# 1/std by a power of -0.5 on GpSimd, for four sets of rows, in a two-layer attention kernel

## The chip, the core and the metric

The kernel runs on one core of a Trainium2 chip. The metric is the time of one execution on the device in microseconds (us), of which the median of several runs is given. Engines are named as in the profile: PE is TensorE, DVE is VectorE, ACT is ScalarE, POOL is GpSimd, SP is SyncE (here it only issues transfers).

## The reference

The input x has 4 batches of 1024 rows of 256 numbers. Four layers are applied, each to rows that are normalised first, and each is added to x. All is in fp32.

```
x = x + attn_a(layernorm(x))      # 16 heads of 64
x = x + ffn(layernorm(x))         # 256 -> 1024 -> 256, exact Gelu
x = x + attn_b(layernorm(x))      # attn_b normalises once more inside, with scale and bias,
                                  # and adds its own normalised input to its output
x = x + ffn(layernorm(x))         # same weights

layernorm: m, v = mean(x), mean((x - m)**2);  (x - m) / sqrt(v + 1e-5)
```

In `attn_b` the inner normalisation has rows that are already normalised, so its variance is the first variance times the square of the first 1/std. Both attentions are softmax(q k^T) v with the heads' outputs multiplied by an output matrix; the second one rotates q and k by position.

## The kernel before

x stays in SBUF for the whole program, as four tiles of 128 partitions with 8 row tiles of 256 columns each. A *block* is half a batch: 512 rows, four row tiles. There are 8 blocks.

**Attention.** `attention` (it is called for both layers) goes through 256 steps: for each of 4 batches, for each of 8 pairs of heads, for each of 8 query tiles. For one step, PE computes the scores of both heads (L238, into PSUM), DVE takes the maximum of each row (L249), ACT the exponential with its row sum (L251), DVE the reciprocal of the sums (L259), ACT copies this into the same tile (L260), and DVE transposes the tile in squares of 32 by 32 (L271). Transfers between SBUF tiles then bring each square to its place (L295): most are issued by SP, five for each two steps by POOL. Some steps later PE multiplies the transposed exponentials by v (L304), ACT copies the sums (L314), POOL multiplies them by the reciprocals (L316), PE projects them (L167), ACT copies the projection (L326) and POOL adds it to x (L328). This second half is done for two steps at a time, so a pair of steps is the period of the work. The order on each engine is written out by hand in `steps_with`; what else has to be done within the attention (the projections of the next pair of heads, the rotation of q and k by POOL in L657 to L659, the normalisation of the next batch) is put into it as *pieces* that each have the number of a step, those of one number in the order in which they were handed in.

**Normalisation.** `scaling` makes tiles for a set of blocks: mean and variance of its rows (`mv`, one column pair for each row tile), `rstd`, `shift` and, for the second attention, `more`. `measure` (L126, L127, DVE) fills `mv`. `finish` works out the factors of the whole set at once: ACT takes the square root (L130), DVE the reciprocal (L131), then DVE the product with the mean and its sign (L137, L138). With `again` the second 1/std follows in the same manner (L133 to L136). `standardize` (L147, ACT) is what uses `rstd` and `shift`: one Identity with a scale and a bias for each row tile.

ACT's functions lie in tables. The program that is built has an `ACT_TABLE_LOAD` ahead of a function whose table isn't there: the square root, the exponential and Gelu each need one of their own; copies and Identity work with each of them.

`Rows` groups the blocks into sets of one layer, each with its own `finish`:

- layer a, `rows` in `layer_a`: block 0, block 1, and blocks 2 to 7. The third set (24 row tiles) is finished as a piece of step 28 of the first attention; its first use is at step 32.
- the two feed-forwards, names f and g: blocks 0 and 1, blocks 2 to 5, blocks 6 and 7. The first set (8 row tiles) is finished at step 254 (`n - 2` in `ffn_between`) of the attention before; `normed(0)` follows it in the same step and uses it at once: four Identities on ACT, each followed by an addition of the bias to x on POOL (L396). Then come transposes on PE (L153), the copies of them (L156), and the first matrix product with Gelu (`up`, L410 and L414).
- layer b, name b: the same sets as f, with `again`. The third set (8 row tiles) is finished at step 30 of the second attention and used for the last batch, from step 152 on.

Of the kernel before, what the change touches and what calls it, by code (L numbers as in the profile page):

```python
# [9 lines left out]
F32 = mybir.dt.float32  # L10
AF = mybir.ActivationFunctionType
ALU = mybir.AluOpType
# [3 lines left out]
P = 128  # L16
# [23 lines left out]
def hybrid_block_kernel(  # L40
# [5 lines left out]
    nc = tc.nc  # L46
# [3 lines left out]
    const = ctx.enter_context(tc.tile_pool(name="const", bufs=1))  # L50
# [26 lines left out]
    make_identity(nc, ident)  # L77
    eps = const.tile([P, 1], F32, name="eps")
    nc.vector.memset(eps, EPS)
    b1_sb = const.tile([P, NF], F32, name="b1_sb")  # L80
    lns_sb = const.tile([P, NC], F32, name="lns_sb")
    lnb_sb = const.tile([P, NC], F32, name="lnb_sb")
# [21 lines left out]
        nc.gpsimd.dma_start(lnb_sb, ln_b.rearrange("(c p) -> p c", p=P))  # L104


    def scaling(name, blocks, again=False):

        where = {}
        for b, qb in blocks:
            for t in range(TQ):
                where[b, qb * TQ + t] = len(where)
        m = len(where)
        mv = const.tile([P, m, 2], F32, name=f"{name}_mv")
        rstd = const.tile([P, m], F32, name=f"{name}_rstd")  # L120
        shift = const.tile([P, m], F32, name=f"{name}_shift")
        more = const.tile([P, m], F32, name=f"{name}_more") if again else None

        def measure(b, t):
            stats = small.tile([P, 6], F32, tag="stats", name="stats")
            nc.vector.bn_stats(stats, xs[b][:, t, :])  # L126
            nc.vector.bn_aggr(mv[:, where[b, t], :], stats)  # L127

        def finish():
            nc.scalar.activation(rstd, mv[:, :, 1], AF.Sqrt, bias=eps)  # L130
            nc.vector.reciprocal(rstd, rstd)  # L131
            if again:
                nc.vector.tensor_mul(more, mv[:, :, 1], rstd)  # L133
                nc.vector.tensor_mul(more, more, rstd)
                nc.scalar.activation(more, more, AF.Sqrt, bias=eps)
                nc.vector.reciprocal(more, more)  # L136
            nc.vector.tensor_mul(shift, mv[:, :, 0], rstd)  # L137
            nc.vector.tensor_scalar_mul(shift, shift, -1.0)  # L138

        def get(b, t):  # L140
            i = slice(where[b, t], where[b, t] + 1)
            return shift[:, i], rstd[:, i], more[:, i] if again else None

        return measure, finish, {k: (lambda k=k: get(*k)) for k in where}

    def standardize(dst, src, shift, rstd):
        nc.scalar.activation(dst, src, AF.Identity, scale=rstd, bias=shift)  # L147

    def transposed(dst, src, c, affine=None):

        tr = group(TQ, P)
        for t in range(TQ):
            nc.tensor.transpose(tr[:, t, :], src[:, t, ts(c, P)], ident)  # L153
        trf = tr.rearrange("p t q -> p (t q)")
        if affine is None:
            nc.scalar.copy(dst[:, c, :], trf)  # L156
        else:
            nc.scalar.activation(
                dst[:, c, :], trf, AF.Identity,
                scale=affine[0][:, c : c + 1], bias=affine[1][:, c : c + 1],  # L160
            )
# [204 lines left out]
    blocks = [(b, qb) for b in range(B) for qb in range(NQB)]  # L366

    class Rows:


        def __init__(self, name, sets, again=False):
            self.finish, self.get, self.by = [], {}, {}
            for i, which in enumerate(sets):
                measure, finish, get = scaling(f"{name}{i}", which, again)
                self.finish.append(finish)
                self.get.update(get)
                self.by.update({k: measure for k in get})
# [114 lines left out]
    def layer_a():  # L492

        scale_a = 1.0 / (DH * DH * H)
        hTs = {}
        rows = Rows("a", (blocks[:1], blocks[1:2], blocks[2:]))

        def batch_a(b):
            work = []
            for qb in range(NQB):  # L500
                k = {}

                def straight(t, b=b, k=k, qb=qb):
                    if t == 0:
                        k["xn"] = xnp.tile([P, TQ, D], F32, tag="xn", name="xn")
                    dst, src = k["xn"][:, t, :], xs[b][:, qb * TQ + t, :]
                    shift, rstd = rows.factors(NQB * b + qb, t)[:2]
                    if b == 0 and qb == 1:
                        nc.vector.tensor_scalar(dst, src, rstd, shift, op0=ALU.mult, op1=ALU.add)
                    else:  # L510
                        standardize(dst, src, shift, rstd)

                def turned(c, b=b, k=k, qb=qb):
                    if c == 0:
                        p, tag = ((lowp, "low"), (highp, f"high{b % 2}"))[qb]
                        hTs[b, qb] = p.tile([P, NC, QB], F32, tag=tag, name="hT")
                    transposed(hTs[b, qb], k["xn"], c)

                work += [(10 * qb + t, lambda t=t, f=straight: f(t)) for t in range(TQ)]
                work += [(10 * qb + 6 + 2 * c, lambda c=c, f=turned: f(c)) for c in range(NC)]  # L520
            return work

        def pair_a(b, pr):
            made = {}

            def load():
                w = made["w"] = wp.tile([P, 3, NC, P], F32, tag="w", name="w")
                for i in (1, 0, 2):
                    nc.gpsimd.dma_start(
                        w[:, i], wqkv_a[i, :, ts(pr, P)].rearrange("(c p) f -> p c f", p=P)  # L530
                    )

            def qk(i, qb):
                name = ("qT", "kT")[i]
                if qb == 0:
                    made[name] = qkp.tile([P, S], F32, tag=name, name=name)
                pq = group(QB)
                paired(pq, [
                    (made["w"][:, i, c, :], [hTs[b, qb][:, c, :]] * 2) for c in range(NC)
                ])  # L540
                dst = made[name][:, ts(qb, QB)]
                if i == 0:
                    nc.scalar.mul(dst, pq, scale_a)
                else:
                    nc.scalar.copy(dst, pq)

            def values(m):
                if m == 0:
                    made["v"] = vp.tile([P, NK2, DH], F32, tag="v", name="v")
                pv = group(4, DH)  # L550
                for t in range(4):
                    qb, tt = divmod(4 * m + t, QB // DH)
                    by_head(pv[:, t, :], [
                        (hTs[b, qb][:, c, ts(tt, DH)], made["w"][:, 2, c, :]) for c in range(NC)
                    ])
                nc.scalar.copy(made["v"][:, ts(m, 4), :], pv)

            work = [(4 - 4 * i + 2 * qb - EARLY, lambda i=i, qb=qb: qk(i, qb)) for i in (1, 0) for qb in range(NQB)]
            work += [(6 + 2 * m, lambda m=m: values(m)) for m in range(NT // 2)]
            return {name: lambda name=name: made[name] for name in ("qT", "kT", "v")}, load, work  # L560


        later = [(4 + i, lambda i=i: rows.measure(2 + i // TQ, i % TQ)) for i in range(6 * TQ)]
        later += [(4 + 6 * TQ, lambda: rows.finish[2]())]
        first, steps = attention(batch_a, pair_a, wo_a, nc.gpsimd, lead=3, kept=0)
        loads, xn, pair = first[:2], first[2:14], first[14:]

        def measured(qb):
            for t in range(TQ):
                rows.measure(qb, t)  # L570
            rows.finish[qb]()

        def ready():

            nc.scalar.activation(small.tile([P, 1], F32, tag="nmax", name="ready"), eps, AF.Exp)


        first = loads + [lambda: measured(0)] + xn[:4] + [lambda: measured(1), ready] + xn[4:6] + pair[:1]
        first += xn[6:] + pair[1:3]
        later += [((-1, 0, 0, 1, 1)[i], f) for i, f in enumerate(pair[3:])]  # L580
        return first, lambda others: steps(later + others)
# [101 lines left out]
    n_steps = B * NF * NT  # L683
    sets = (blocks[:2], blocks[2:6], blocks[6:])
    first_a, steps_a = layer_a()
    rows_b = Rows("b", sets, again=True)
    first_b, steps_b = layer_b(rows_b)
    end_a, rest_a, ramp_b = ffn_between(Rows("f", sets), False, n_steps, rows_b, first_b)
    end_b, rest_b, _ = ffn_between(Rows("g", sets), True, n_steps)
    for f in first_a[:2]:  # L690
        f()
    load_rest()
# [63 lines left out]
```

## Time and profile before

| | |
|---|---|
| three runs | 3285.77, 3290.56, 3292.66 us; median 3290.56 |
| the profiled execution | 3286.08 us, of which 3284.2 are the span from the first to the last instruction |
| first attention and its start | about 0 to 1415 us |
| first feed-forward | about 1415 to 1560 us |
| second attention | about 1560 to 3030 us |
| second feed-forward | about 3030 to 3284 us |
| granted PE clock | 0.997 of full, mean over the span |
| ACT_TABLE_LOAD | 20, of 1283 ns each |
| square roots, L130 and L135 | 15, of about 0.3 us each |
| DVE reciprocals, L131 and L136 | 15, of 0.18 to 0.30 us each |

The first layers of the next stage overlap the end of the one before, so the limits of the stages are not sharp. In the profile's lines a time is given in us from the start of the span; an operation is named by its engine, its line in the kernel, what it writes and what it reads. Text in square brackets says how long the engine stood idle before it, and what ended that. Busy time of POOL is rough, and a PE that is shown busy isn't at its peak.

### The profile page before, as it was taken

How to read it: one execution, taken by the hardware profiler on the slowest of the kernel's cores; microseconds unless marked ns; L12 is line 12 of the kernel's file. 1: busy time of each engine (PE TensorE's matmuls, PEld its weight loads, DVE VectorE, ACT ScalarE, POOL GpSimd, SP SyncE). 2: the span in 40 equal slices, each digit the busy share in tenths (PEclk: the TensorE clock that was granted, in tenths of full speed). 3: DMA queues.
4: the chain of work that ended last, by engine and by line, in shares of the span. 5: the costliest groups of instructions: out<-in, count | busy, mean ns of one | idle time of the engine just before them, and what ended most of it. 6: DMA issues, size and time to landing. Idle time of an engine off the chain costs nothing.

```text
span 3284.2 us, 126564 instructions
## 1 busy us (share of the span) xinstructions
PE 3204.3 (98%) x52736; PEld 2022.2 (62%) x52736; DVE 2531.7 (77%) x2386; ACT 2107.9 (64%) x4304; POOL 1958.5 (60%) x2738
## 2 busy tenths in 40 slices
PE   8999999999999999999999999999999999998999
PEld 4666666666666666666555556666666666655666
DVE  7988888888888888941049889998999899998100
ACT  5666666666666666643447877787777777777332
POOL 4545454445544544430158889998889898986110
PEclk9999999999999999999999999999999999999999
DMA  8888888888888888840039889988888899987100
GB/s 227 226 218 219 223 225 221 221 220 229 222 216 217 224 221 227 216 112 1 4 87 238 222 222 243 244 240 231 237 237 239 232 246 244 241 240 212 39 20 20
DMA packets 244698, 642.13 MB, mean 196 GB/s; under 512 B 74305, under 2 KB 102977, under 8 KB 244129
## 3 DMA queue, kind: packets, MB, share of 16 engines
q1 hardware_dynamic: 161104, 397.60, 47.4%
q0 software_dynamic: 83024, 236.44, 25.6%
q8 instruction: 419, 6.86, 1.0%
q14 instruction: 151, 1.23, 0.1%
HBM read 43.39 MB, written 4.19 MB: 14 GB/s over the span
## 4 chain that ended last, share of the span: by engine, by line
PE 71%; SPq 12%; DMA 6%; DVE 4%; ACT 4%; issue 3%; POOL 1%; DVEq 0%; ACTq 0%; POOLq 0%
PE sc L238 20%; PE mm L304 19%; PE mm L167 15%; SPq L295 11%; PE mm L421 7%; PE ph L410 7%; DMA pT<-T 5%; PE mm L176 4%; DVE T L271 2%; DVE nmax L249 1%; ACT p L251 1%; POOL oT L316 1%; PE mm L153 1%; ACT gT L414 0%; SPq L636 0%
## 5 line engine op out<-in xcount | busy, mean ns | idle before, releaser
L249 DVE TENSOR_REDUCE nmax<-sc 128x1 f32<-128x1024 f32 x1024 | 1204.3, 1218 | 222.8 <-PE sc L238 219.7
L251 ACT ACTIVATE p<-sc,nmax 128x1024 f32<-128x1024 f32 x1024 | 1144.1, 1117 | 323.0 <-DVE nmax L249 323.0
L271 DVE STREAM_TRANSPOSE T<-p 128x2176 f32<-128x2176 f32 x512 | 1247.4, 2436 | 50.9 <-DMA pT<-T 24.6
L238 PE MATMUL sc<-kT,qT 64*64 64x512 f32 x8192 | 1087.2, 598 | 15.6 <-ACT p L251 10.5
L304 PEld LDWEIGHTS mm<-pT,v 64*64 64x64 f32 x32768 | 951.3, 133 | 141.7 <-issue 100.6
L304 PE MATMUL mm<-pT,v 64*64 64x128 f32 x32768 | 986.7, 269 | 10.3 <-issue 9.5
L295 POOL DMA_DIRECT2D pT<-T x1280 | 629.6, 499 | 120.8 <-PE sc L238 55.4
L316 POOL TENSOR_TENSOR oT<-oT,pT 128x256 f32<-128x256 f32 x256 | 186.2, 727 | 719.7 <-ACT oT L314 647.7
L238 PEld LDWEIGHTS sc<-kT,qT 64*64 64x64 f32 x8192 | 333.8, 133 | 413.8 <-issue 276.1
L328 POOL TENSOR_TENSOR x<-x,got 128x512 f32<-128x512 f32 x256 | 330.9, 1293 | 26.9 <-ACT got L326 22.9
L326 ACT COPY got<-mm 128x512 f32<-128x512 f32 x256 | 149.8, 585 | 282.0 <-PE mm L167 282.0
L428 DVE TENSOR_TENSOR x<-x,mm 128x512 f32<-128x512 f32 x32 | 22.0, 687 | 367.1 <-PE mm L421 367.1
L167 PE MATMUL mm<-wo,oT 128*64 128x256 f32 x2048 | 278.4, 393 | 19.9 <-POOL oT L316 18.7
L167 PEld LDWEIGHTS mm<-wo,oT 128*64 128x64 f32 x2048 | 124.6, 136 | 267.3 <-POOL oT L316 221.5
L260 ACT COPY p<-total 128x128 f32<-128x128 f32 x512 | 151.8, 297 | 203.7 <-DVE total L259 197.1
L414 ACT ACTIVATE gT<-ph,b_sb 128x512 f32<-128x512 f32 x128 | 87.4, 685 | 299.6 <-PE ph L410 299.5
L167 PE MATMUL mm<-hT,w 128*64 128x512 f32 x1024 | 243.3, 596 | 1.1 <-ACT hT L156 1.0
L421 PE MATMUL mm<-w_sb,gT 128*128 128x256 f32 x1024 | 226.0, 381 | 6.5 <-ACT hT L156 6.5
L410 PE MATMUL ph<-hT,w_sb 128*128 128x512 f32 x512 | 229.3, 601 | 0.2 <-ACT hT L156 0.2
L421 PEld LDWEIGHTS mm<-w_sb,gT 128*128 128x128 f32 x1024 | 193.1, 190 | 39.4 <-ACT hT L156 9.4
L396 POOL TENSOR_TENSOR x<-x,b_sb 128x256 f32<-128x256 f32 x64 | 44.5, 726 | 275.5 <-ACT xn L147 275.5
L251 ACT ACTIVATION_READ_ACCUMULATOR p<-sc,nmax 128x1 f32 x1024 | 205.0, 200 | 0.0
(90 smaller groups left out, 2471.4 us busy)
## 6 DMA issues: line engine op xcount, KB each, us to landing
pT<-T SPq DMA_DIRECT2D x2688, 136.0 KB, 4.7
pT<-T POOLq DMA_DIRECT2D x1280, 136.0 KB, 4.8
turned<-kT POOLq DMA_DIRECT2D x128, 128.0 KB, 3.5
turned<-qT POOLq DMA_DIRECT2D x128, 128.0 KB, 3.3
w<-in_wqkv_a POOLq DMA_DIRECT2D x96, 128.0 KB, 5.9
wo<-in_wo_a POOLq DMA_DIRECT2D x32, 128.0 KB, 5.1
wo<-in_wo_a POOLq DMA_DIRECT2D x64, 64.0 KB, 5.3
wo<-in_wo_b SPq DMA_DIRECT2D x32, 128.0 KB, 3.7
```

The source lines that it names most:

```text
L167: nc.tensor.matmul(out[ts(j, DH)], lhsT[:, ts(j, DH)], rhs[j], start=(first and i == 0), stop=(last and i == len(parts) - 1),)
L238: nc.tensor.matmul(sc[s, j][ts(half, DH), ts(m, 512)], qT()[rows, ts(2 * qs + half, DH)], kT()[rows, ts(m, 512)], start=True, stop=True,)
L249: nc.vector.tensor_reduce(nmax, sc[s, j], AX.X, ALU.max, negate=True)
L251: nc.scalar.activation(probs[s][:, :NK2, ts(j, 2), :], sc.pop((s, j)).rearrange("p (k c i) -> p k c i", c=2, i=SQ), AF.Exp, bias=nmax, acc ...
L260: nc.scalar.copy(probs[s][:, NK2].rearrange("p (j c) i -> p j (c i)", j=2), t.unsqueeze(2).to_broadcast([P, 2, DH]),)
L271: nc.vector.transpose(T[h][:, :, q, :, :].rearrange("p c k i -> p k c i"), probs.pop(s))
L295: engine.dma_start(pT[h][ts(c, SQ), a], T[h][ts(a, SQ), c])
L304: nc.tensor.matmul(av[h][q][ts(j ^ q, DH)], v[ts(j, DH), k, :], pT[h][ts(j, DH), :, q, k, :], start=(k == 0), stop=(k == NK2 - 1),)
L316: nc.gpsimd.tensor_mul(parts, parts, pT.pop(h)[:, :, :, NK2, :])
L328: nc.gpsimd.tensor_add(xd, xd, got)
L410: nc.tensor.matmul(ph, w1_sb[:, c, ts(f, P)], hT[n][:, c, :], start=(c == 0), stop=(c == NC - 1),)
L421: nc.tensor.matmul(po[n][:, t % 2, :], gT[n][:, f, ts(t, P)], w2_sb[:, f, :], start=(f == 0), stop=(f == NF - 1),)
```

## The change

`scaling` gets an argument `apart`. Where it is set, all that `finish` did is done by POOL instead: eps is added to the variance, and the sum is raised to the power of -0.5 by a tile operation whose second operand is a new tile `half` of one column that holds -0.5, read for all columns; the products follow on POOL too. With `again` the second 1/std is worked out in the same manner. `apart` is set for four of the twelve sets: the third of layer a, the third of layer b, and the first of each feed-forward. The other eight sets keep the square root on ACT and the reciprocal on DVE.

```diff
     eps = const.tile([P, 1], F32, name="eps")
     nc.vector.memset(eps, EPS)
+    half = const.tile([P, 1], F32, name="half")
+    nc.vector.memset(half, -0.5)
...
-    def scaling(name, blocks, again=False):
+    def scaling(name, blocks, again=False, apart=False):
...
+        def power(dst, var):
+
+            nc.gpsimd.tensor_add(dst, var, eps.to_broadcast([P, m]))
+            nc.gpsimd.tensor_tensor(dst, dst, half.to_broadcast([P, m]), op=ALU.pow)
+
+        def finish_apart():
+            power(rstd, mv[:, :, 1])
+            if again:
+                nc.gpsimd.tensor_mul(more, mv[:, :, 1], rstd)
+                nc.gpsimd.tensor_mul(more, more, rstd)
+                power(more, more)
+            nc.gpsimd.tensor_mul(shift, mv[:, :, 0], rstd)
+            nc.gpsimd.tensor_scalar_mul(shift, shift, -1.0)
+
         def finish():
+            if apart:
+                return finish_apart()
             nc.scalar.activation(rstd, mv[:, :, 1], AF.Sqrt, bias=eps)
             nc.vector.reciprocal(rstd, rstd)
...
-        def __init__(self, name, sets, again=False):
+        def __init__(self, name, sets, again=False, apart=()):
...
-                measure, finish, get = scaling(f"{name}{i}", which, again)
+                measure, finish, get = scaling(f"{name}{i}", which, again, i in apart)
...
-        rows = Rows("a", (blocks[:1], blocks[1:2], blocks[2:]))
+        rows = Rows("a", (blocks[:1], blocks[1:2], blocks[2:]), apart=(2,))
...
-    rows_b = Rows("b", sets, again=True)
+    rows_b = Rows("b", sets, again=True, apart=(2,))
...
-    end_a, rest_a, ramp_b = ffn_between(Rows("f", sets), False, n_steps, rows_b, first_b)
-    end_b, rest_b, _ = ffn_between(Rows("g", sets), True, n_steps)
+    end_a, rest_a, ramp_b = ffn_between(Rows("f", sets, apart=(0,)), False, n_steps, rows_b, first_b)
+    end_b, rest_b, _ = ffn_between(Rows("g", sets, apart=(0,)), True, n_steps)
```

## The prediction

> **What bounds the kernel now.** I read the page first. TensorE is busy for 98% of the span, and it owns 71% of the chain that ended last. ScalarE (64%) and GpSimd (60%) have room on average, so removing their work is worth something only where TensorE waits for it.
>
> ```profile
> PE 3204.3 (98%) x52736; PEld 2022.2 (62%) x52736; DVE 2531.7 (77%) x2386; ACT 2107.9 (64%) x4304; POOL 1958.5 (60%) x2738
> PE 71%; SPq 12%; DMA 6%; DVE 4%; ACT 4%; issue 3%; POOL 1%; DVEq 0%; ACTq 0%; POOLq 0%
> ```
>
> The four changed places are, in order of time: a (third set of layer a, step 28 of the first attention, 183 us), f (first set of the first feed-forward, step 254, 1417 us), b (third set of layer b, step 30 of the second attention, 1850 us) and g (as f, 3030 us). Next I followed the chain of waits through the stretch around each. At a it leaves TensorE and passes the square root with its table, VectorE's part, and the table that brings the exponential back:
>
> ```profile
> 183.40 1.28 ACT L130
> ...
> 184.69 0.32 ACT a_rstd L130
> ...
> 185.04 0.32 DVE a_rstd L131
> ...
> 186.25 1.28 ACT L251
> ...
> 190.25 0.73 POOL oT L316
> ...
> 191.03 2.80 PE mm L167 x16
> ```
>
> Columns: start, length, what. The output projection (L167) starts at 178.58, 191.03 and 201.78. A pair of steps normally takes 10.75 us, this one 12.45. So **a loses 1.70 us**, although 3.8 us of ScalarE's and VectorE's time lie in the chain.
>
> The stretches with the granted clock add what the chain doesn't name:
>
> ```profile
> 1419.00:1422.00 3.00, 0.19 (x3) 0.00 (x0) 0.67 (x5) 2.43 (x7) 1.75 (x3) 1.00 0.99 242
> ...
> 1424.00:1427.00 3.00, 3.00 (x5) 1.30 (x4) 2.83 (x12) 1.32 (x2) 2.10 (x5) 0.50 0.44 100
> ...
> 3035.00:3038.00 3.00, 3.00 (x10) 2.16 (x10) 2.93 (x6) 2.66 (x4) 1.81 (x4) 0.50 0.05 13
> ...
> 1857.00:1859.00 2.00, 1.85 (x11) 0.63 (x14) 1.84 (x2) 2.00 (x7) 0.41 (x1) 0.54 0.13 34
> ```
>
> After the bounds and length come the busy times of PE, PEld, DVE, ACT and POOL; third from the end is the clock. At f, b and g TensorE stands idle (2.86, 2.33 and 3.20 us) and then runs at half clock for some 3 us.
>
> **What the change removes.** One table load each at f and g (the Gelu table is still loaded), two each at a and b: six loads of 1283 ns, 7.7 us; five square roots of 0.3 us; five reciprocals and ten small VectorE operations. The skill's "ScalarE: Activation LUTs", section "What ACT_TABLE_LOAD costs", adds a drain of some 1380 ns to each load, 16 us in all. Here the load at 183.40 follows a copy that ended at 183.38, and the square root starts 10 ns after the load. No drain shows; I use 1283 ns.
>
> **What it adds.** On GpSimd four dependent operations at a, f and g, eight at b, all of 8 columns except a's 24; and one memset on VectorE at the start, under its 3.96 us wait for the input (free; about 0.06 us, as the one of eps, if it weren't). An ordinary GpSimd operation is priced from two rows:
>
> ```profile
> L328 POOL TENSOR_TENSOR x<-x,got 128x512 f32<-128x512 f32 x256 | 330.9, 1293 | 26.9 <-ACT got L326 22.9
> L316 POOL TENSOR_TENSOR oT<-oT,pT 128x256 f32<-128x256 f32 x256 | 186.2, 727 | 719.7 <-ACT oT L314 647.7
> ```
>
> (1293 - 727)/256 = 2.21 ns a column and 161 ns fixed, so 0.18 us for 8 columns and 0.21 for 24. Between dependent ones lie 0.07 us (the rotation's L658 to L659), and from a GpSimd result to another engine 0.33 us (L316 ends at 1412.98, L167 starts at 1413.31).
>
> **The power** is in no row. From below: it costs what an add does, 0.18 us. From above, the skill's "GPSIMD Engine Reference", section "Performance pitfalls for Q7 kernels", speaks against the change: a dependent fp32 chain costs 4 cycles per element and step at 1.2 GHz, 3.3 ns. With some 30 steps for a logarithm and an exponential (my guess), that is 0.1 us a column: an estimate of 0.96 us for 8 columns, 2.6 for 24. No run here shows it. I take p = 0.3 us for 8 and 0.6 for 24, near the only measured rows. By the rule the sum below becomes 3.5 to 5 us instead of 8.
>
> **a.** GpSimd's residual add ends at 182.57; then come 3 x 0.21 + 4 x 0.07 + 0.6 = 1.5 us, and behind them three loads of w (2.2 us), which are needed at step 32, 16 us later (they take 5.9 to land), and then the attention's product L316. Before that GpSimd idles 5.42 us, of which 1.70 go with the stall: 3.7 us of cover. The factors themselves are first used at step 32. VectorE no longer waits 1.63 us for the root. Gain **1.7**; it shrinks from a power of 2.8 us (24 columns) on.
>
> **f.** The residual add ends at 1417.07; 3 x 0.18 + 4 x 0.07 + 0.3 + 0.33 = 1.45 us, so the normalisation can start at 1418.5 instead of 1419.57. TensorE's idle time falls from 2.86 to 1.8 us, and three pauses of 1.73, 2.00 and 2.84 us elsewhere (2281.9, 46.6 and 2985.2) left the clock at 1.00. But something else is late next:
>
> ```profile
> 1425.39 1.28 ACT L414 ACT_TABLE_LOAD   x1 [1.58 <-DMA pT<-T]
> ```
>
> The first Gelu writes where a transposed block was, and waits until its transfers have landed. SyncE issues them one after another, not moved by the change. The first Gelu would end at 1427.4 instead of 1427.65, and since only three score buffers can be filled ahead of it, the clock's 2 us are mostly lost here. Then the faster matmuls win back a little by the projection at 1430.42. Gain **0.4** (0.2 to 1).
>
> **b.** L167 starts at 1844.55 and 1860.69: 16.14 us where 10.05 would do, 6.1 lost (1.9 of it the half clock: 14 L238 matmuls took 3.61 instead of some 1.7). GpSimd, 89% busy around here, has nearly no cover:
>
> ```profile
> 1851.82 1.27 POOL L659 TENSOR_TENSOR qT<-qT,turned 128x512 f32<-128x512 f32 x1
> 1858.59 0.72 POOL L316 TENSOR_TENSOR oT<-oT,pT 128x256 f32<-128x256 f32 x1 [5.50 <-ACT oT L314]
> ```
>
> Its 5.50 us of idleness are the stall itself. The eight operations stand between these two lines: 6 x 0.18 + 8 x 0.07 + 2 x 0.3 = 2.2 us from 1853.09. L316 starts at 1855.3 instead of the 1853.8 of an undisturbed pair, and L167 at 1856.2. TensorE idles about 1.7 us instead. Behind L316 stand GpSimd's two copies for the rotation and five of the transposes' transfers; those are used 15 us later, and the next L316 (due at 1866) is met: 1856.1 + 1.1 + 2.4 + 1.3 + 3.9 = 1864.8. Gain **4.4**, less 2 us per us of power, and 1.9 less if the clock falls again.
>
> **g.** As f: the add ends at 3029.99, the normalisation starts at 3031.4 instead of 3032.28, 0.84 earlier. TensorE's pause falls from 3.2 to 2.4 us, which may keep the clock or not (2.33 at b lost it, 2.84 at 2985 kept it). No transfer holds the Gelu here. With the full clock the projection at 3042.68 would come at 3040.6, a gain of 2.1; with the half, 0.84. I take **1.5**. Behind f and g the feed-forwards are TensorE's, so the gain stays.
>
> **Sum:** 1.7 + 0.4 + 4.4 + 1.5 = 8.0 us. The profiled execution took 3286.1 us (3284.2 of span and 1.9 around it), so 3278.1; it lies 4.5 below the median of the three runs, 3290.56, from which I count: **3282.5**.
>
> **Rivals.** *Given back:* the power costs near 1 us, and GpSimd stalls b's projection by 2.8 us, with half clock. Then a 1.7, f 0.2, g 0.2, b 1.4: 3.5 us, 3287. For it: GpSimd's 89%, and a queue stop of 2.87 us at 1883 that led to a TensorE pause of 3.28. Against it: the idle 5.4 us at a, and the short fixed cost in the rows. *Slow power:* GpSimd is in order, so a long power holds L316 at a and b and the normalisation at f and g. The gain is gone at p = 1.5 us for 8 columns (a 0.3, f -0.1, g -0.4, b 0.3). At 5 us (14.7 for 24) it is -10.2 - 3.6 - 3.9 - 6.7 = -24: **3315**. [...]against it: nothing in the trace. *Not as said:* the tables are loaded all the same, say behind another square root: 3290 or slightly more.
>
> **Chances.** Forecast 0.40, given back 0.24, slow power 0.33, not as said 0.03. About 0.2% (6.6 us) is what a measurement of this kernel can tell from no change. The forecast clears it by little; 0.85 of it and 0.15 of "given back" are faster: 0.38. Slower is the slow power, less the part near break-even, and a little of "given back": 0.32. The same: 0.30. The forecast's own range is 3278 to 3287, and that for 8 in 10 goes from 3276 (cheap power, clock kept everywhere, 0.1% of scatter) to 3318.
>
> **What would show it.** Table loads fall from 20 to 14; the power's row gives p at once; the pair at a takes 10.75 us; at b L316 follows the last new operation and L167 starts some 11.7 us after the one before; at f the Gelu still waits for the transfer; the clock stays at 1.00 at f. I'd be wrong if the power took over 1.5 us, if TensorE's pause at b weren't GpSimd's, or if later pairs of the second attention gave the gain back.

## The result, and the profile after

The changed kernel takes **3305.33 us** (median of 5 runs, 3301.83 to 3312.34), the kernel before 3287.81 us (5 runs, 3285.77 to 3292.66). The ratio is 1.0055, with a 95% interval of 1.0043 to 1.0066. That is 17.5 us slower in the medians, where 8 us less were forecast. (The prediction counted from the median of three of these five runs, 3290.56 us.)

The profiled execution took 3301.83 us, with a span of 3300.1. The page's lines on busy time and on the chain that ended last:

```profile
PE 3210.3 (97%) x52736; PEld 2018.6 (61%) x52736; DVE 2527.8 (77%) x2372; ACT 2099.5 (64%) x4293; POOL 1972.4 (60%) x2758
PE 64%; SPq 16%; DMA 7%; DVE 4%; issue 4%; ACT 3%; POOL 2%; DVEq 0%; POOLq 0%; ACTq 0%
```

The busy times are the same within 1%, and ScalarE lost 8 us of it, as it should (14 table loads of 1283 ns instead of 20, so the rival "not as said" is out). But the chain has moved: TensorE's share fell from 71 to 64%, and the queue of SyncE, which does nothing but issue transfers, went from 12 to 16%. The change edits no transfer.

The power is in the groups of instructions. Columns: line, engine, operation, what it writes and reads, count, busy us and mean ns of one, idle time before it:

```profile
L135 POOL TENSOR_TENSOR a_rstd<-a_rstd,half 128x24 f32<-128x24 f32 x1 | 4.2, 4194 | 0.1
L135 POOL TENSOR_TENSOR f_rstd<-f_rstd,half 128x8 f32<-128x8 f32 x1 | 1.7, 1675 | 0.1
```

So the time of one power, the prediction's p, is 1.67 us for 8 columns and 4.19 for 24: (4194 - 1675)/16 = 157 ns a column, and 0.42 us fixed. The other new operations cost 0.19 to 0.28 us.

What that does at the four places can be read directly. At a, the chain of waits after (start, length, what):

```profile
189.67 1.79 PE sc L257 x16
...
191.50 0.72 POOL w L548
...
192.24 0.74 POOL oT L335
...
193.03 2.80 PE mm L186 x16
```

The table loads are gone from the chain; in their place stand GpSimd's load of w, which the power pushed back, and the product behind it. The projection before this one starts at 180.63, so the pair takes 12.40 us; it took 12.45. At b, the timeline (start, length, engine, line, what; in brackets the idle time before):

```profile
1854.74 1.28 POOL L678 TENSOR_TENSOR qT<-qT,turned 128x512 f32<-128x512 f32 x1
1856.26 1.67 POOL L135 TENSOR_TENSOR b_rstd<-b_rstd,half 128x8 f32<-128x8 f32 x1
1858.85 1.63 POOL L135 TENSOR_TENSOR b_more<-b_more,half 128x8 f32<-128x8 f32 x1
1861.15 0.72 POOL L335 TENSOR_TENSOR oT<-oT,pT 128x256 f32<-128x256 f32 x1 [0.17 <-issue]
1861.93 1.08 PE L186 MATMUL mm<-wo,oT 128*64 128x256 f32 x8 [3.18 <-POOL oT L335]
```

The eight operations stand between the rotation and the product, as foretold, and TensorE waits 3.18 us for them. Before, it waited 2.33 us for ScalarE and then ran at half clock; now it waits longer, and the clock falls again:

```profile
1424.00:1427.00 3.00, 3.00 (x10) 2.00 (x9) 2.93 (x6) 1.17 (x2) 1.81 (x3) 0.50 0.30 80
...
3050.00:3054.00 4.00, 3.35 (x11) 1.92 (x12) 3.76 (x7) 3.66 (x7) 2.81 (x5) 0.63 0.20 49
...
1862.00:1866.00 4.00, 4.00 (x20) 1.73 (x24) 1.51 (x1) 2.71 (x5) 3.98 (x8) 0.65 0.72 196
```

(f, g and b; the clock is third from the end.) One wait took the place of the other. But that explains no loss. To find it I put the start of each of the 256 products L316 (after: L335) of the two traces beside each other, and took the differences of the stretches between them, in us:

| stretch (products) | before | after | difference |
|---|---|---|---|
| first attention, 0 to 9 | 98.1 | 99.9 | +1.9 |
| a, 9 to 15 | 66.2 | 66.1 | -0.1 |
| first attention, 15 to 123 | 1179.1 | 1179.0 | -0.1 |
| f, 123 to 127 | 48.3 | 48.7 | +0.4 |
| feed-forward and start of the second attention, 127 to 138 | 373.4 | 373.8 | +0.5 |
| b, 138 to 144 | 71.0 | 70.2 | -0.8 |
| **second attention, 144 to 251** | 1120.9 | 1134.2 | **+13.3** |
| g, 251 to 255 | 46.9 | 47.5 | +0.5 |

The four changed places together make no difference. The time is lost in 107 pairs of the second attention, in which not one instruction was changed. The queues' part of the trace, for the 1000 us from 1900 to 2900, before and then after. The columns are packets, MB, and the time of the packets as a share of 16 DMA engines; q1 is the queue of SyncE, q0 that of GpSimd:

```profile
q1 hardware_dynamic: 63592, 144.33, 55.9%
q0 software_dynamic: 32095, 91.59, 32.1%
```

```profile
q1 hardware_dynamic: 62393, 141.92, 56.9%
q0 software_dynamic: 31684, 90.44, 33.0%
```

Fewer packets take more time. One of q1 took 0.559 x 16 x 1000 / 63592 = 0.1407 us on the mean and takes 0.1459; one of q0 took 0.160 and takes 0.167. Both are about 4% more. So the transfers themselves became slower. And what the diff does to all of them at once is this: the tile `half` is allocated ahead of nearly every other tile. It has 4 bytes per partition and takes up 32, and in the layout of the program all tiles behind it start 32 bytes later. The blocks of exponentials T and pT, between which L295 (after: L314) transfers, began at multiples of 256 bytes; now they begin 32 bytes after one.

### The profile page after: what moved, and what is told of

The parts are those of the page before. It is cut to its first block, busy times and chain, and to the rows that moved or that the text cites. A ratio compares the mean times of both kernels' runs of the same rounds, so it can differ in the third digit from the quotient of the medians.

```text
span 3300.1 us, 126559 instructions
## 1 busy us (share of the span) xinstructions
PE 3210.3 (97%) x52736; PEld 2018.6 (61%) x52736; DVE 2527.8 (77%) x2372; ACT 2099.5 (64%) x4293; POOL 1972.4 (60%) x2758
## 3 DMA queue, kind: packets, MB, share of 16 engines
HBM read 43.39 MB, written 4.19 MB: 14 GB/s over the span
## 4 chain that ended last, share of the span: by engine, by line
PE 64%; SPq 16%; DMA 7%; DVE 4%; issue 4%; ACT 3%; POOL 2%; DVEq 0%; POOLq 0%; ACTq 0%
PE sc L257 17%; PE mm L323 16%; SPq L314 14%; PE mm L186 13%; PE mm L440 7%; DMA pT<-T 7%; PE ph L429 7%; PE mm L195 4%; DVE T L290 2%; DVE nmax L268 2%; ACT p L270 1%; POOL oT L335 1%; SPq L655 1%; PE mm L172 0%; SPq L233 0%
## 5 line engine op out<-in xcount | busy, mean ns | idle before, releaser
L257 PE MATMUL sc<-kT,qT 64*64 64x512 f32 x8192 | 1088.4, 598 | 13.3 <-ACT p L270 8.6
L314 POOL DMA_DIRECT2D pT<-T x1280 | 629.9, 499 | 123.0 <-PE sc L257 60.9
L335 POOL TENSOR_TENSOR oT<-oT,pT 128x256 f32<-128x256 f32 x256 | 186.0, 727 | 712.2 <-ACT oT L333 630.1
L433 ACT ACTIVATE gT<-ph,b_sb 128x512 f32<-128x512 f32 x128 | 87.5, 686 | 301.0 <-PE ph L429 300.9
```

The costliest lines, as they stand in the source:

```text
L257: nc.tensor.matmul(sc[s, j][ts(half, DH), ts(m, 512)], qT()[rows, ts(2 * qs + half, DH)], kT()[rows, ts(m, 512)], start=True, stop=True,)
L314: engine.dma_start(pT[h][ts(c, SQ), a], T[h][ts(a, SQ), c])
L335: nc.gpsimd.tensor_mul(parts, parts, pT.pop(h)[:, :, :, NK2, :])
```

## The experiments

**Theory "layout":** the transfers became slower because tiles no longer start at multiples of 256 bytes, and the second attention is paced by them. **Rival "order":** the power at step 30 upsets the order on GpSimd, and the second attention stays in a slower rhythm. Each was timed beside the kernel before, and all edits but those of e4, e7 and e8 are to the kernel before.

**e1: the tile alone.**

```diff
+    half = const.tile([P, 1], F32, name="half")
+    nc.vector.memset(half, -0.5)
```

> The kernel before with nothing of the change but the tile of -0.5 and its memset; no set is finished on GpSimd. In the layout that the program is given, the new tile takes 32 bytes per partition, and every tile behind it (T and pT among them) starts 32 bytes later. Theory 'layout' (transfers between tiles that no longer start at a multiple of 256 bytes are slower, and the second attention is paced by them): about 3303 us, 1.005 of before, the DMA queues' share up from 47.4 and 25.6% to about 48.8 and 26.4%. Theory 'order' (GpSimd's power at step 30 leaves the second attention in a slower rhythm): 3288 us, as before, shares as before.

Measured: 3310.17 us, 1.0061 (1.0049 to 1.0074). One unused tile makes the whole loss, with all square roots where they were. The shares are 48.4 and 26.3%. Products 144 to 251 take 1141 us. "Order" is out as the cause of the loss.

**e2, e9, e3: the same tile with 64, 128 and 256 bytes.**

```diff
+    half = const.tile([P, 16], F32, name="half")
+    nc.vector.memset(half, -0.5)
```

(e2; in e9 the tile has 32 columns, in e3 it has 64.)

> As the run with the tile only, but the tile is 64 bytes wide, so T and pT start 64 bytes behind a multiple of 256. Layout with a bound at 256 bytes: as slow as with 32 bytes, about 3303 us. Layout with a bound at 64 bytes: 3288 us. Order: 3288 us.

Measured: 3303.39 us, 1.0041 (1.0029 to 1.0054). The interval overlaps that of e1, so that 64 bytes cost less than 32 isn't shown.

> As the run with the tile only, but the tile is 128 bytes wide, so T and pT start 128 bytes behind a multiple of 256. If only multiples of 256 keep the writes of pT quick: about 3303 us, 1.004 to 1.006. If multiples of 128 are enough: 3288 us.

Measured: 3298.18 us, 1.0021 (1.0012 to 1.0030). Neither expectation came true: the loss is a third of e1's, and the fifteen runs fall into two groups, seven from 3288.77 to 3293.32 us and eight from 3298.18 to 3303.58. The median is the lowest of the upper group. The profiled run is one of the lower group, 3290.81 us.

> As the run with the tile only, but the tile is 256 bytes wide, so every later tile keeps its place against multiples of 256. Layout: 3288 us, as before, and the DMA shares as before. If any other place in memory were enough to slow the transfers: about 3303 us. Order: 3288 us.

Measured: 3288.42 us, 0.9996 (0.9987 to 1.0004); shares 47.3 and 25.7%. So it isn't the presence of another tile, nor any move: a tile and memset that move the others by 256 bytes cost nothing, a move by 32, 64 or 128 costs time.

**e4: the whole change without the move.** Both constants lie in the 32 bytes that eps took alone.

```diff
-    eps = const.tile([P, 1], F32, name="eps")
-    half = const.tile([P, 1], F32, name="half")
+    two = const.tile([P, 2], F32, name="eps")
+    eps, half = two[:, 0:1], two[:, 1:2]
```

> The whole change, but -0.5 lies beside eps in one tile of two columns, so that every other tile stays where it was before. Layout: the four places alone remain; with a power of 1.67 us for 8 and 4.19 for 24 columns my sum gives a +0.3, f -0.2, g -0.5, b about 0: 3287 to 3290 us, the same as before. Order: about 3304 us, as the change.

Measured: 3288.48 us, 1.0000 (0.9992 to 1.0009). The change itself is worth nothing, within 0.1%. By the products' starts it makes +0.4 us at a, -1.1 at f, -0.7 at b and +0.9 at g. All but g's lie within the scatter: in the six kernels here that leave the four places as they were (e1, e2, e3, e5, e6, e9), the same stretches differ from before by -0.3 to +0.4, -1.5 to +2.2, -1.3 to +0.3 and -0.1 to +0.5, in this order.

**e5, e6: which end of the transfers.** L295 reads T and writes pT. Two unused tiles move one of them by 32 bytes and put everything behind it back in step.

```diff
     tp = pool("T", 2)
+    gap0 = pool("gap0", 1).tile([P, 8], F32, name="gap0")
+    nc.vector.memset(gap0, 0.0)
     ptp = pool("pT", 2)
+    gap1 = pool("gap1", 1).tile([P, 56], F32, name="gap1")
+    nc.vector.memset(gap1, 0.0)
```

(e6; in e5 they stand around T.)

> The kernel before with two unused tiles of 32 and 224 bytes around T, so that T alone starts 32 bytes behind a multiple of 256; pT and all other tiles keep their place against it. If the reading end of the transfers pT<-T is what the place matters for: about 3303 us, as the run with the tile only. If the writing end: 3288 us. If both: about half, 3295 us.

Measured: 3288.80 us, 1.0001 (0.9993 to 1.0009).

> The same around pT: pT alone starts 32 bytes behind a multiple of 256, T and all others keep their place. Reading end: 3288 us. Writing end: about 3303 us. Both: about 3295 us. If neither this nor the run with T moved is slow, the loss comes from other transfers (the rotation's turned<-qT, the weights).

Measured: 3304.99 us, 1.0055 (1.0040 to 1.0070). The queues from 1900 to 2900 us, e5 and then e6:

```profile
q1 hardware_dynamic: 63362, 143.64, 55.0%
q0 software_dynamic: 32064, 91.51, 31.4%
```

```profile
q1 hardware_dynamic: 62349, 141.79, 57.4%
q0 software_dynamic: 31584, 90.14, 33.2%
```

By the same sum a packet of q1 takes 0.139 us in e5, a little less than before, and 0.147 in e6; one of q0 takes 0.157 and 0.168. In e6 both are about 5% more than before. So it is the writing end, and pT alone makes the whole loss. No engine is slower at reading the moved pT: the products with v take 269 ns and GpSimd's product 727 ns on the mean before and in e6 alike.

The traces also tell packets apart by size. Those of 4352 bytes are the transfers from T to pT, 32 for each. Over the whole run they take 258.7 to 263.0 ns on the mean in the six kernels with pT in its old place or 256 bytes on (before, e3, e4, e5, e7, e8), and 268.0 to 273.0 in the five with pT moved otherwise (the change, e1, e2, e6, e9). The stretch of products 144 to 251 takes 1120.9 to 1126.4 us in the first six and 1133.5 to 1141.2 in the change, e1, e2 and e6. In e9's trace it takes 1127.5, although its packets are slow, too (268.0): slower transfers need not become lost time.

The Trainium skill, "DMA: Bandwidth & Descriptors", section "How a descriptor splits into AXI transactions", has a rule of this kind: a transfer is split into pieces of at most 256 bytes, each of which has to start at a multiple of 256. A square of pT has 2 x 17 x 32 x 4 = 4352 bytes per partition, 17 pieces of 256 if it starts at such a multiple, and 18 by the page's rule if it doesn't. That makes an estimate of 5.9% more time, if each piece costs the same; the runs show 4 to 5% in this stretch. But the page speaks of reading, where e5 shows no loss, and the loss is in the writing. And the count would be 18 with 64 and 128 bytes as well, though e9 loses a third of what e1 loses. So that the number of pieces is the cause is not shown; the runs show the place and the size.

**e7: the four places with a cheap operation.** Layout as in e4.

```diff
-            nc.gpsimd.tensor_tensor(dst, dst, half.to_broadcast([P, m]), op=ALU.pow)
+            nc.gpsimd.tensor_tensor(dst, dst, half.to_broadcast([P, m]), op=ALU.mult)
```

> The whole change in the layout of before, with a product in place of the power, so that the factors are -(v + eps)/2 and not 1/std: it costs an ordinary 0.18 to 0.21 us. If my sum for the four places is right and only the power was mis-sized: 8.2 us less than before, 3281 us, 0.9975. If the four places can't give time at all (it is lost again later in the attention): 3288 us, as with the power.

Measured: 3277.03 us, 0.9968 (0.9960 to 0.9976), some 11 us less. The factors are wrong in this kernel, so it shows a time and nothing else. At the places: a -1.6, f -3.5, b -4.8, g -2.1. The gain that the layout and a dear power hid was there, and more of it at f. The timeline there:

```profile
1417.13 0.20 POOL L135 TENSOR_TENSOR f_rstd<-f_rstd,eps 128x8 f32<-128x8 f32 x1
...
1421.78 5.42 PE L429 MATMUL ph<-hT,w_sb 128*128 128x512 f32 x12 [0.24 <-ACT hT L175]
...
1425.62 1.28 ACT L433 ACT_TABLE_LOAD   x1 [3.40 <-DMA pT<-T]
...
1427.13 1.08 PE L186 MATMUL mm<-wo,oT 128*64 128x256 f32 x8
```

The Gelu does wait for the transfer, 3.40 us now, but TensorE doesn't wait for the Gelu: its twelve records end and the projection starts at 1427.13, before the first Gelu (L433, from 1426.91 on) has ended.

**e8: the power under cover.** Layout as in e4. Layer a's 24 row tiles become three sets, the feed-forwards' first sets are finished four steps earlier, layer b's chain is cut in four.

```diff
-        rows = Rows("a", (blocks[:1], blocks[1:2], blocks[2:]), apart=(2,))
+        rows = Rows("a", (blocks[:1], blocks[1:2], blocks[2:4], blocks[4:6], blocks[6:]), apart=(2, 3, 4))
...
-        later += [(4 + 6 * TQ, lambda: rows.finish[2]())]
+        later += [(4 + 2 * TQ * (i + 1), lambda i=i: rows.finish[2 + i]()) for i in range(3)]
...
-        ends += [(n - 2, lambda: rows.finish[0]()), ...
+        ends += [(n - 6, lambda: rows.finish[0]()), ...
...
-            ] + [(30, lambda: nxt.finish[2]())]
+            ] + [(30 + 10 * i, f) for i, f in enumerate(nxt.parts[2])]
```

(`parts` has the operations of `finish_apart`: the power, the two products for the second variance, the second power, the shift.)

> The whole change in the layout of before, with its work put where GpSimd has cover: layer a's 24 row tiles in three sets of 8, finished at steps 12, 20 and 28; the feed-forwards' first set at step 250 instead of 254; layer b's two powers apart, in four parts at steps 30, 40, 50 and 60. If GpSimd's cover is what decides: a +1.7, f +0.7, g +3.4, b about +4, so 3279 us, 0.997. If the time comes back as waits elsewhere: 3288 us.

Measured: 3273.45 us, 0.9956 (0.9941 to 0.9971): **14.5 us less than before**, the lowest median here. At the places: a -1.5, f -3.5, b -5.2, g -3.4. At b a single power now stands in the way of the product:

```profile
1844.98 1.67 POOL L135 TENSOR_TENSOR b_rstd<-b_rstd,eps 128x8 f32<-128x8 f32 x1
1846.63 0.72 POOL L343 TENSOR_TENSOR oT<-oT,pT 128x256 f32<-128x256 f32 x1
```

The product before starts at 1835.41, so this pair takes 11.2 us instead of 14.84. TensorE doesn't fall to half clock at f, b or g: its granted clock is 1.00 in every stretch of 2 us from 1396 to 1440, from 1830 to 1870 and from 2996 to 3040. What the earlier steps alone would bring, with the square root still on ScalarE, was not run.

## Why the prediction was wrong

**The step that failed** is "one memset on VectorE at the start, under its 3.96 us wait for the input", which the prediction called free. The new tile was priced as an instruction, and not as a place in memory. What it displaced makes the whole loss: the tile alone costs 1.0061, and without its move the change stands at 1.0000. That this is 1.0000 and not the forecast 8 us less is a second step that failed, the size of p. The measured time lies within the range of 3276 to 3318 us by luck: the upper end stood for a slow power, and no term of the prediction stands for the layout.

**The power** was mis-sized: 0.3 us was taken for 8 columns, 0.6 for 24; it costs 1.67 and 4.19. It lies beyond even the prediction's estimate by the dependent steps of the Trainium skill's "GPSIMD Engine Reference", section "Performance pitfalls for Q7 kernels" (0.96 and 2.6). That an ordinary operation was the nearest measured row was no reason to think that this one cost as little. With the measured p the sum's own terms give +0.3 us at a, -0.2 at f, -0.5 at g and about 0 at b, and e4 shows -0.4, +1.1, -0.9 and +0.7 (gains): break-even at p = 1.5 us was about right. That agrees in the sum; the single values are near the scatter given with e4. The rival "slow power" therefore named rightly how the gain was lost, and at nearly the right p; its 3315 us, worked out for p = 5 us, lie near the measured time for another reason, the layout, which no rival had.

**a, b and g** were right for a cheap operation: forecast 1.7, 4.4 and 1.5 us, e7 shows 1.6, 4.8 and 2.1. That GpSimd has cover at a and none at b holds too: at a the power of 24 columns exceeded the 3.7 us, and at b L335 follows the last new operation directly.

**f** was wrong: 0.4 us forecast, 3.5 in e7. The wait of the Gelu for its transfer was foretold rightly, and so was its end. What failed is the step from there to TensorE: that the clock's 2 us are lost because only three score buffers can be filled ahead of the Gelu. Three are enough. Before, this stood ahead of the projection:

```profile
1423.38 7.11 PE L410 MATMUL ph<-hT,w_sb 128*128 128x512 f32 x12 [0.24 <-ACT hT L156]
...
1430.42 1.08 PE L167 MATMUL mm<-wo,oT 128*64 128x256 f32 x8
```

A page has 512 such records (x512) for 2 x 8 x 8 x 2 = 256 products of the program, so a product leaves two. A group is two products, so the twelve records are three groups, one for each buffer, and the projection needs no Gelu. In e7 the twelve start 1.60 us earlier and take 5.42 us instead of 7.11, and both gains come through whole.

**The scatter** of 0.1% held for the medians. A long stretch differs by 4 to 6 us between the traces of the six kernels with pT in place (products 15 to 123: 1175.7 to 1179.9 us; 144 to 251: 1120.9 to 1126.4), so of a single trace's difference there only the coarse size counts. The +1.9 us at the start of the first attention can be of this kind, for e7 has +1.4 there in the layout of before. But e1, e2 and e9 have +1.1 to +2.6, so that a small effect of the layout there isn't excluded.

**Open:** why e9 falls into two groups of times with slow packets in the quicker one, and why the second attention loses so much more than the first. In the first, q1's packets of 4352 bytes grow as much (271.6 to 281.5 ns between 200 and 1000 us). The queues are 88% busy in the second before and 85% in the first, so the share alone hardly says it.

## What to carry to other kernels

Before a tile is added, look at which tiles lie behind it and where transfers into them start: a tile of a few bytes goes into a slot that is already padded, or is widened until the others keep their place. An operation that no row shows is best measured alone before its place is chosen; then put it where its engine has idle time of that length ahead of the next instruction that others wait for. And when the changed places show no loss, compare the traces stretch by stretch: the cause may lie where nothing was edited.

## What the runs showed of the hardware

- Transfers of 4352 bytes per partition between SBUF tiles took about 5% longer per packet in the second attention when the tile that they write (pT) started 32 bytes behind a multiple of 256, and the kernel 0.55% longer (e6). With everything moved by 32 bytes the kernel took 0.61% longer, by 64 bytes 0.41%, by 128 bytes 0.21% (in two groups of runs), by 256 none. At the reading end (T) 32 bytes cost nothing (1.0001).
- The first attention loses little by it: products 15 to 123 take 1179.0 to 1182.6 us in the change, e1, e2 and e6, against 1175.7 to 1179.9 with pT in place. The second loses some 13 us.
- A power on GpSimd costs about 0.42 us and 157 ns a column of 128 rows (two points, 8 and 24 columns), where ordinary sums and products cost 2.2 ns a column.
- A power of 1.67 us put where GpSimd has cover costs no time that the runs can tell: e8 (0.9956) is not slower than e7 with its cheap operation (0.9968), though e8 also moves the work.
